# Later signs in the last block, a folded softmax sum, separate tiles for two convolution sums, and two matmul rounds moved ahead of a wait

## The chip, the cores and the metric

The kernel runs on one core of one Trainium2 chip. The metric is the time of one execution on the device in microseconds (us); the time before is 1892.93 us, the median of three runs from 1892.58 to 1893.13. The engines are named as in the profile: PE is TensorE (matmuls; PEld its weight loads), DVE is VectorE, ACT is ScalarE, POOL is GpSimd, SP is the engine whose queue issues most DMAs.

## The reference

The input x has 8 images of 64 channels and 64 x 64 pixels, float32. Two layers follow each other.

```
# layer 0: attention over the N = 4096 pixels of each image
q, k, v = wq @ x + bq, wk @ x + bk, wv @ x + bv
q, k = q - mean(q), k - mean(k)                       # means over pixels
out = softmax(q^T k / 8) applied to v  +  a unary term, one column per image
x = x + out
# layer 1: three binary convolutions and a gate
for kernel sizes 1, 3, 5:
    s += batchnorm(conv(sign(x + move), sign(w - mean(w)) * mean(|w|)))
gate = sigmoid(grouped linear map of the mean of s over pixels)   # one value per channel
out = s * gate + x
```

The gate needs the mean of s over the whole image, so no pixel of an image can be written before all of its convolutions have been summed, in one form or another.

## The kernel before

Two images lie on the 128 partitions (64 channels each), so there are four pairs of images. A pair's 4096 query pixels are cut into 8 blocks of 512 (8 image rows each); `attend` runs the 32 blocks one after the other.

**The rounds of a block.** A block has 32 rounds, one for each 128 keys. In a round `scores` makes the logits (L584) into a pair of PSUM banks, ScalarE takes their exponential into a tile `e` (L597; the pool `ep` has five of these), `weighted` multiplies the `e` of the round before with the values (L609) into the two banks `acc`, and `summed` adds the `e` of the round before to the running sum `es` on VectorE (L627, called a fold below). `weighted` and `summed` are one round behind `scores`.

**The plan.** Everything else is woven into the rounds by `plan`: `put(i, f, ...)` lists the function f to be issued in round i. For block g, the plan holds the steps that finish block g-1: the softmax sums go through DRAM (`gather`, `fold_first`, `fold`, `fold_last`, `spread`), then `added` (L719) joins the two halves of the attention output, `finish` (L723, L724) scales it and adds x, `signs_wide` (L762) and `signs` (L756) write the signs for the three convolutions on ScalarE and start the DMAs that copy them to the other image's partitions (L840, L757). Each engine works through its own queue in the order in which the instructions are issued, so a step's round decides what is queued behind it.

**The last block.** Block 31 is done in two parts, `PARTS`: a wide part of 384 query columns in 32 rounds, and a narrow part of 128 columns in 8 rounds of four key tiles each. `plan_last` takes the plan of block 31 and moves index i to i * 512 // 384, then puts its own steps. `NK` is 32, so `NK + n` is round n of the narrow part.

For the last pair the gate must be known before the convolutions of the last rows are summed. So the mean of s over rows 40 to 63 is taken from sums of signs along image rows: `row_sums(n, y0, y1)` reduces the signs of convolution n (0, 1, 2 for sizes 1, 3, 5) over rows y0 to y1 (L789) and corrects the ends (L795), and `gate_lines` multiplies these line sums with all taps (L809). `gate_mean` (L1125, L1127) sums what the earlier rows gave; `gate_lines_out` (L822), `gate_logits` and `gate_out` make the gate from both.

**The tail.** After the last round: `sums_wide` (L698) multiplies ones with the running sum `es` and with the last `e` to get the softmax sums of the narrow part; `reciprocals_wide` (L713) inverts them; the last `weighted` group follows, and `added_out` and `finish` give the last 128 pixels (rows 62 and 63). TensorE then runs the convolutions of blocks 5 and 6 (rows 40 to 55): `one` for the 1x1, `three` with 9 rounds and `five` with 25 rounds of four matmuls each, one round per tap (L1099). `out1` and `add` (L1113, L1118) bring them from PSUM into the sums; `store` (L1159) applies the gate and starts the output DMA. Last come rows 56 to 63 (block 7), for which the 3x3 and the 5x5 sums lie side by side in one PSUM tile of two banks:

```
t = ps_s.tile([P, 2, QB], F32, tag="s", name=f"z{p.name}_7")
w = QB // 2
z5, z3 = t[:, :, 0:w], t[:, :, w:]
```

L1557 adds all of z3 in one instruction, L1558 applies the gate, L1561 adds the 5x5 sums in two halves, and each half is stored by a DMA (L1563).

Of the kernel before, what the change touches and what calls it, by code (L numbers as in the profile page):

```python
# [18 lines left out]
F32 = mybir.dt.float32  # L19
# [3 lines left out]
ALU = mybir.AluOpType  # L23
# [3 lines left out]
P = 128  # L27
C = 64
HH = 64
N = HH * HH  # L30
KS = (1, 3, 5)
QB = 512
NQ = N // QB
NK = N // P
ROWS = QB // HH
# [13 lines left out]
def conv_seq_kernel(ctx, tc, x, wqv, wk, wv, w1, w3, w5, wtap, gw, out):  # L49
    nc = tc.nc  # L50
    n_pairs = x.shape[0] * x.shape[1] // P
    xf = x.rearrange("b c h w -> (b c) (h w)")
    of = out.rearrange("b c h w -> (b c) (h w)")
# [9 lines left out]
    ps_s = ctx.enter_context(tc.tile_pool(name="ps_s", bufs=2, space=PSUM))  # L63
# [3 lines left out]
    def m_tile(name):  # L67
        return ps_m.tile([P, QB], F32, tag="m", name=name)
# [4 lines left out]
    def load_x(name, rows, queues=(nc.sync,)):  # L73
        xt = x_tile(name)
        for c in range(4):
            cols = bass.ts(c, N // 4)
            queues[c % len(queues)].dma_start(out=xt[:, cols], in_=xf[rows, cols])
        return xt
# [118 lines left out]
    scale = cp.tile([P, 3], F32, tag="scale", name="scale")  # L197
# [82 lines left out]
    class Pair:  # L280
# [407 lines left out]
                )  # L688


        def sums_wide(self, qb, part=(slice(0, QB), 1), more=None):
            cols, n = part
            w = cols.stop - cols.start
            sums = m_tile(f"su_{self.name}_{qb}_{cols.start}")
            es = [self.es.pop(qb)] + ([] if more is None else [more])
            for i in range(n * len(es)):
                for b in range(2):
                    nc.tensor.matmul(  # L698
                        sums[img[b], 0:w],
                        ones[:, 0:C],  # L700
                        es[i // n][:, b, i % n * w : (i % n + 1) * w],
                        start=(i == 0),
                        stop=(i == n * len(es) - 1),
                    )
            self.sums_p = sums, cols.start

# [575 lines left out]
    def banks(pool, tag):  # L1282
        def two(name):
            t = pool.tile([P, 2, QB], F32, tag=tag, name=name)
            return [t[:, 0, :], t[:, 1, :]]

        return two

    quarters = [slice(c * N // 4, (c + 1) * N // 4) for c in range(4)]
    score_banks = banks(ps_s, "s")  # L1290
# [4 lines left out]
    def acc_banks(name):  # L1295
        return [ps_a.tile([P, QB], F32, tag=f"acc{h}", name=f"{name}_{h}") for h in range(2)]
# [5 lines left out]
    def rows_of(pr):  # L1302
        return slice(pr * P, (pr + 1) * P)

    def attend(pairs, early):
# [3 lines left out]
        def block(g):  # L1309
            return pairs[g // NQ], g % NQ  # L1310
# [4 lines left out]
        def plan(g):  # L1315


            at = {}

            def put(i, f, *a):  # L1320
                at.setdefault(i, []).append((f, a))

            pr, qb = divmod(g, NQ)
# [4 lines left out]
            if g >= 1:  # L1328
                p, b = block(g - 1)
# [28 lines left out]
            if g >= 1:  # L1358
                put(5, p.fold_first, b)
                put(6, p.fold, b)  # L1360
                put(7, p.fold_last, b)
                put(8, p.spread, b)
                put(9, p.check_block, b, 0)
                put(11, p.check_block, b, 1)
                last = g == n_blocks - 1
                put(11 if last else 13, p.added, b)
                put(12 if last else 15, p.finish, b)
                put(13 if last else 16, p.signs_wide, b, 2)
                put(13 if last else 18, p.signs_wide, b, 1)
                put(14 if last else 20, p.signs, b)  # L1370
            if g + 2 < n_blocks:
                put(2, lambda: block(g + 2)[0].copy_x(block(g + 2)[1], (g + 2) // NQ * P))
            if 2 <= g < n_blocks - 1:
# [33 lines left out]
            if pr + 1 < n_pairs:  # L1407
# [10 lines left out]
                if qb == 3:  # L1418
                    for c in range(8):
                        cols = slice(c * QB, (c + 1) * QB)  # L1420
                        put(14 + 2 * c, lambda c=c, cols=cols: nx().mean_part(c, cols, True))
                    put(30, lambda: nx().mean_sum(8))
                if qb >= 4:
                    for h in range(2):
                        i = 2 * (qb - 4) + h
# [8 lines left out]
        def plan_last():  # L1434

            at, (first, _) = {}, PARTS
            for i, steps in plan(n_blocks - 1).items():
                at[i * QB // first[0].stop] = steps

            def put(i, f, *a):  # L1440
                at.setdefault(i, []).append((f, a))

            p, b = pairs[-1], NQ - 1
            cols = first[0]
            r1 = cols.stop // HH
            put(4, p.begin_lines)
            for i, n in enumerate((2, 1, 0)):
                put(5 + i, p.row_sums, n, L0 - pads[n], 48)
                put(19 + i, p.row_sums, n, 48, 56)
            put(24, p.gate_mean)  # L1450
            put(NK, p.weighted_out, b, cols)
            put(NK + 1, p.added, b, cols)
            put(NK + 1, p.sums_wide, b, first)
            put(NK + 1, p.reciprocals_wide, b, cols)
            put(NK + 2, p.finish, b, cols)
            put(NK + 3, lambda: p.check(p.r[b][:, cols], n_blocks - 1))
            put(NK + 4, p.signs_wide, b, 2, 0, r1)
            put(NK + 5, p.signs_wide, b, 1, 0, r1)
            put(NK + 5, p.row_sums, 2, 56, 56 + r1)
            put(NK + 6, p.signs, b, 0, r1)  # L1460
            return at

        for g in range(n_blocks):
            pr, qb = divmod(g, NQ)
            last = g == n_blocks - 1
            at = plan_last() if last else plan(g)
            p = pairs[pr]
            parts = PARTS if last else ((slice(0, QB), 1),)
            steps = [(part, j) for part in parts for j in range(NK // part[1])]
            for i, (part, j) in enumerate(steps):  # L1470
                first = g == 0 and j < len(early)
                e = early[j] if first else p.scores(qb, j, None, part)
# [10 lines left out]
        p, b = pairs[-1], NQ - 1  # L1483

        def run(rounds):
            for f in rounds:
                f()

        part = PARTS[1]
        cols = part[0]  # L1490
        r0, r1 = cols.start // HH, ROWS
        y0, y1 = N // HH - ROWS + r0, N // HH
        rows_p = rows_of(n_pairs - 1)
        p.sums_wide(b, part, pending[1][2])
        p.row_sums(1, N // HH - ROWS, y0)
        p.row_sums(0, N // HH - ROWS, y0)
        p.reciprocals_wide(b, cols)
        pending[0].weighted(*pending[1], pending[2])
        z1, z5 = score_banks(f"z{p.name}_1"), score_banks(f"z{p.name}_5")
        z3 = []  # L1500
        halves = p.rows(NQ - 3), p.joint_rows(0, ROWS)
        one, three, five, out1, add = p.last_rows(halves, z1, z3, z5)
        one()
        p.added_out(b, cols)
        for side in range(2):
            p.check(p.r[b][:, cols], n_pairs * (NQ + 1), (side,))
        p.finish(b, cols)
        z3 += acc_banks(f"z{p.name}_3")
        run(five[0:2])
        run(three)  # L1510
        nb_ = sm.tile([P, 1], F32, tag="nb", name="nb")
        nc.vector.tensor_reduce(nb_, fit, AX.XY, ALU.add)
# [11 lines left out]
        out1(1)  # L1524
        add(1, 0)
        p.gate_lines_out()
        run(five[2:4])
        p.gate_logits()
        pb = m_tile("pb")
        nc.tensor.matmul(pb[:, 0:1], ones, nb_, start=True, stop=True)  # L1530
        run(five[4:])
        add(1, 1)
        good = sm.tile([P, 1], I32, tag="good", name="good")
        nc.vector.tensor_copy(good, pb[:, 0:1])
# [1 line left out]
        by = sm.tile([P, 1], F32, tag="nb", name="by")  # L1536
# [4 lines left out]
            add(2, h)  # L1541
            p.store(NQ - 3 + h, rows_p)

        t = ps_s.tile([P, 2, QB], F32, tag="s", name=f"z{p.name}_7")
        w = QB // 2
        z5, z3 = t[:, :, 0:w], t[:, :, w:]
        z1 = m_tile(f"z{p.name}_7_1")
        for i in range(2):
            p.conv_tap(p.joint_rows(ROWS, 2 * ROWS), [[z1]], i, 0, 0, 0, True, True)
        halves = [p.joint_rows(ROWS + h * ROWS // 2, ROWS + (h + 1) * ROWS // 2) for h in range(2)]  # L1550
        _, three, five, *_ = p.last_rows(halves, None, [z3[:, h] for h in range(2)], [z5[:, h] for h in range(2)])
        run(three)
        run(five)
        s = p.s[NQ - 1]
        nc.scalar.activation(s, z1, AF.Identity, bias=shift, scale=scale[:, 0:1])
        sv = s.rearrange("p (h w) -> p h w", w=w)
        nc.vector.scalar_tensor_tensor(sv, z3, scale[:, 1:2], sv, ALU.mult, ALU.add)  # L1557
        nc.vector.scalar_tensor_tensor(s, s, p.gt, p.x2[NQ - 1], ALU.mult, ALU.add)  # L1558
        for h in range(2):
            sh = sv[:, h, :]  # L1560
            nc.vector.scalar_tensor_tensor(sh, z5[:, h, :], by, sh, ALU.mult, ALU.add)  # L1561
            at = N - QB + h * w
            nc.sync.dma_start(out=of[rows_p, at : at + w], in_=sh)  # L1563
        return good

    with tc.manual_schedule():
# [30 lines left out]
        first.early_unary()  # L1597
        mix((first, 1), None)
        good = attend([first] + [None] * (n_pairs - 1), early)


# [3 lines left out]
    with tc.If(n_good < P):  # L1605
        neg = fp.tile([P, QB], F32, tag="t5", name="neg")
        nc.vector.memset(neg, 0.0)
        with tc.For_i(0, n_pairs * P, P) as row:
            rows = bass.ds(row, P)
            p = Pair("g", load_x("g", rows, (nc.scalar,)))  # L1610
# [11 lines left out]
            for qb in range(NQ):  # L1622
                mix((p, qb), None)
                for h in range(QB // P):
                    part = sm.tile([P, 2, NQ], F32, tag="part", name=f"part_{qb}_{h}")
                    for kb_ in range(NQ):
                        ps = ps_s.tile([P, 2, QB], F32, tag="s", name=f"px_{qb}_{h}_{kb_}")
                        for b in range(2):
# [5 lines left out]
                                stop=True,  # L1634
# [12 lines left out]
                for j in range(NK):  # L1647
                    e = p.scores(qb, j, neg)
# [75 lines left out]
```

## Time and profile before

| what | value |
|---|---|
| median of three runs | 1892.93 us |
| the profiled execution, its own time | 1892.65 us |
| its span, first to last instruction | 1890.8 us |
| PE busy | 1874.5 us, 99% |
| DVE busy | 1608.7 us, 85% |
| ACT busy | 1265.6 us, 67% |
| POOL busy | 130.1 us, 7% |
| mean granted TensorE clock | 0.999 |
| HBM traffic | 68 GB/s over the span |

A busy TensorE here means that a matmul was in flight. The page also follows the chain of work that ended last back to the start: TensorE holds 90% of it, and the two largest lines are L584 and L609, the attention's matmuls, with 43% each. Stretches of the last 111 us (busy us of each engine and number of instructions in it, granted clock, share of the DMA engines, GB/s):

```profile
1800.00:1820.00 20.00, 19.88 (x334) 9.81 (x330) 17.49 (x32) 13.71 (x20) 0.86 (x1) 1.00 0.27 55
1820.00:1840.00 20.00, 16.13 (x184) 7.18 (x179) 18.92 (x32) 11.21 (x19) 0.00 (x0) 0.91 0.11 32
1840.00:1850.00 10.00, 10.00 (x132) 4.71 (x124) 7.58 (x11) 6.25 (x8) 0.00 (x0) 1.00 0.01 2
1850.00:1860.00 10.00, 10.00 (x275) 7.64 (x268) 7.27 (x10) 5.97 (x7) 2.35 (x1) 1.00 0.02 4
1860.00:1870.00 10.00, 9.69 (x313) 9.13 (x308) 8.65 (x13) 6.81 (x12) 0.00 (x0) 1.00 0.13 30
1870.00:1880.00 10.00, 10.00 (x243) 6.62 (x238) 8.34 (x27) 3.73 (x11) 1.47 (x5) 1.00 0.27 97
1880.00:1891.00 11.00, 3.89 (x138) 3.62 (x128) 5.27 (x8) 0.78 (x1) 0.00 (x0) 0.92 0.31 113
```

The columns after the stretch and its length are PE, PEld, DVE, ACT and POOL. The wide part of the last block runs from about 1804 to 1853, the narrow part to about 1867, and the tail from there.

### The profile page before, as it was taken

What the parts mean: (1) busy time and instruction counts of PE and PEld (TensorE: products, weight loads), DVE (VectorE), ACT (ScalarE), POOL (GpSimd) and SP (SyncE); (2) the same over time, 40 slices, a digit from 0 to 9 for tenths busy, and PEclk for the clock granted to TensorE, in tenths of its full rate; (3) what the DMA queues carried; (4) which work ended last, traced back from release to release, by engine and by line L of the source; (5) the groups of instructions that cost most, each with busy time, mean ns of one, the idle gap of its engine ahead of it and who ended that gap; (6) DMA issues with size and microseconds to landing.
All of it is one profiled execution on the core that took longest, in us unless ns stands there. A gap on an engine that the chain in (4) does not pass through costs nothing.

```text
span 1890.8 us, 51550 instructions
## 1 busy us (share of the span) xinstructions
PE 1874.5 (99%) x22088; PEld 796.0 (42%) x22088; DVE 1608.7 (85%) x2548; ACT 1265.6 (67%) x1622; POOL 130.1 (7%) x176
## 2 busy tenths in 40 slices
PE   9999999999999999999999999999999999999998
PEld 4344344343344434443434444444433344444446
DVE  7888888889888888888888898888888888888887
ACT  6666776666666676666666667666666666666664
POOL 0000000000000000000000000000000000000000
PEclk9999999999999999999999999999999999999999
DMA  4234333333333433233333444233333333333311
GB/s 127 64 68 97 82 66 72 67 58 72 67 71 88 117 82 82 65 73 66 58 72 67 94 115 89 58 81 67 71 68 57 73 78 88 89 72 66 84 37 54
DMA packets 74004, 142.81 MB, mean 76 GB/s; under 512 B 10540, under 2 KB 42152, under 8 KB 73640
## 3 DMA queue, kind: packets, MB, share of 16 engines
q0 software_dynamic: 22320, 81.27, 23.3%
q1 hardware_dynamic: 51160, 57.58, 10.4%
q8 instruction: 174, 2.85, 0.6%
q10 hardware_dynamic: 288, 0.60, 0.1%
q14 instruction: 62, 0.51, 0.1%
HBM read 39.27 MB, written 89.78 MB: 68 GB/s over the span
## 4 chain that ended last, share of the span: by engine, by line
PE 90%; DMA 1%; ACT 0%; DVE 0%; issue 0%; ACTq 0%; DVEq 0%
PE ps L584 43%; PE acc L609 43%; PE z L968 2%; DMA es<-e 1%; PE z L1099 1%; PE pv L416 1%; PE pq L565 1%; PE z_5e L968 0%; ACT e L597 0%; PE su L698 0%; DVE es L627 0%; PE z L1058 0%; PE po L463 0%; PE zl L809 0%; ACT s L762 0%
## 5 line engine op out<-in xcount | busy, mean ns | idle before, releaser
L597 ACT ACTIVATE e<-ps 128x1024 f32<-128x1024 f32 (+1 forms) x1030 | 1047.6, 1017 | 566.9 <-PE ps L584 548.7
L627 DVE TENSOR_TENSOR es<-es,e 128x1024 f32<-128x1024 f32 (+1 forms) x841 | 1018.8, 1211 | 194.7 <-ACT e L597 181.7
L609 PE MATMUL acc<-e,v 64*64 64x512 f32 (+2 forms) x8432 | 1084.9, 577 | 6.2 <-ACT e L597 6.2
L584 PE MATMUL ps<-q,x 64*64 64x512 f32 (+2 forms) x8448 | 1089.6, 578 | 0.8 <-DVE q L349 0.8
L609 PEld LDWEIGHTS acc<-e,v 64*64 64x64 f32 x8432 | 333.3, 131 | 553.6 <-ACT e L597 321.0
L584 PEld LDWEIGHTS ps<-q,x 64*64 64x64 f32 x8448 | 357.0, 133 | 485.2 <-issue 264.1
L648 POOL DMA_DIRECT2D es<-e x93 | 80.0, 861 | 905.1 <-ACT e L597 600.0
L1038 DVE SCALAR_TENSOR_TENSOR sb<-pt,sb 128x256 f32<-128x256 f32 x174 | 65.9, 419 | 0.0
L968 PEld LDWEIGHTS <-wc 64*64 64x64 bf16 x3364 | 58.8, 106 | 1.7 <-issue 0.8
L648 POOL DMA_DIRECT2D es<-es x31 | 26.6, 857 | 438.7 <-DVE es L627 438.7
L625 DVE TENSOR_TENSOR es<-e,e 128x1024 f32<-128x1024 f32 (+1 forms) x31 | 37.7, 1216 | 17.2 <-ACT e L597 17.2
L968 PE MATMUL z<-ec,wc 64*64 64x128 bf16 x1392 | 51.4, 217 | 0.0
L968 PE MATMUL z<-t,wc 64*64 64x128 bf16 x1392 | 51.0, 216 | 0.1
L762 ACT ACTIVATE s<-x,wqv_s 128x512 bf16<-128x512 f32 (+2 forms) x66 | 46.1, 702 | 3.6 <-DVE x L724 3.5
L1001 ACT ACTIVATE pt<-z,frac 128x256 f32<-128x256 f32 (+1 forms) x58 | 30.5, 577 | 16.9 <-PE z L968 16.9
L646 POOL DMA_DIRECT2D es<-e x31 | 17.5, 564 | 334.2 <-ACT e L597 323.0
L635 DVE COPY o<-acc 128x512 f32<-128x512 f32 (+1 forms) x32 | 22.0, 687 | 9.8 <-PE acc L609 9.7
L1012 DVE TENSOR_TENSOR pt<-pt 128x384 f32<-128x384 f32 x58 | 29.6, 552 | 0.0
L416 PEld LDWEIGHTS pv<-wx,x 64*64 64x64 f32 x992 | 21.5, 134 | 16.1 <-issue 8.6
L663 DVE TENSOR_TENSOR e_parts<-e_parts 128x512 f32<-128x512 f32 x31 | 21.3, 687 | 6.6 <-DMA e_parts<-es 6.6
L724 DVE SCALAR_TENSOR_TENSOR x<-x,ou,x 128x512 f32<-128x512 f32 (+2 forms) x33 | 24.3, 735 | 1.2
L424 ACT COPY v<-pv 128x512 f32<-128x512 f32 x31 | 18.2, 586 | 8.7 <-PE pv L416 8.7
(206 smaller groups left out, 888.7 us busy)
## 6 DMA issues: line engine op xcount, KB each, us to landing
es<-e POOLq DMA_DIRECT2D x124, 512.0 KB, 5.1
es<-es POOLq DMA_DIRECT2D x31, 512.0 KB, 5.2
e_parts<-es SPq DMA_DIRECT2D x124, 128.0 KB, 2.9
r<-rc SPq DMA_DIRECT2D x62, 128.0 KB, 2.8
out<-sb SPq DMA_DIRECT2D x29, 256.0 KB, 2.2
x<-in_x SPq DMA_DIRECT2D x24, 256.0 KB, 4.1
ec<-t SPq DMA_DIRECT2D x29, 99.0 KB, 4.5
xc<-in_x SPq DMA_DIRECT2D x30, 72.0 KB
```

The costliest lines, as they stand in the source:

```text
L416: nc.tensor.matmul(pv[img[h], b, i * w : (i + 1) * w], self.x[img[b], bass.ds((4 * g + i) * P + h * H, H)], self.wx[img[b], 0:w], start=Tr ...
L584: nc.tensor.matmul(ps[img[h], b, i * w : (i + 1) * w], self.x[img[b], bass.ds((n * j + i) * P + h * H, H)], self.q[qb][img[b], cols], star ...
L597: nc.scalar.activation(e, ps[:, :, 0 : n * w], AF.Exp, scale=1.0 / 8.0)
L609: nc.tensor.matmul(self.acc[qb][h][img[b], 0:w], self.v[img[h], t, img[b]], e[img[h], b, at : at + w], start=(t == 0), stop=(t == NK - 1),)
L625: begin.tensor_tensor(self.es[qb], self.first, e, ALU.add)
L627: nc.vector.tensor_tensor(self.es[qb], self.es[qb], e, ALU.add)
L648: nc.gpsimd.dma_start(out=out, in_=e, accum_op=ALU.add)
L762: nc.scalar.activation(sy[n][0][:, rows, pad : pad + HH], self.x2[qb][:, r0 * HH : r1 * HH].rearrange("p (h w) -> p h w", w=HH), AF.Sign, ...
L968: nc.tensor.matmul(z[img[b], :].rearrange("p (q w) -> p q w", w=HH), wc[k][img[h], n, c * C : c * C + C], src[:, first : first + step + 1 ...
L1001: nc.scalar.activation(out, z, AF.Identity, scale=frac[:, by : by + 1])
L1012: nc.vector.tensor_tensor(self.pairs[:, :, :, r, :], t[:, 0:3, 0], t[:, 0:3, 1], op)
L1038: nc.vector.scalar_tensor_tensor(out, x, by, out, ALU.mult, ALU.add, **gap)
```

## The change

All of it lies in the last block and the tail; the other 31 blocks are issued as before.

- **Signs at later rounds.** For block 31's plan, `finish` goes from index 12 to 13, the 5x5 signs from 13 to 15, the 3x3 signs from 13 to 16, the 1x1 signs from 14 to 17; `added` stays at 11. In rounds these are 16 to 17, 17 to 20, 17 to 21 and 18 to 22. The row sums of rows 48 to 55 go from rounds 19, 20, 21 to 22, 23, 24, and `gate_mean` from 24 to 18. The row sums of the 5x5 signs of rows 56 to 61 go from round 5 of the narrow part to round 6.
- **A folded sum.** A new function, `fold_parts`, adds on VectorE the four quarters of `es` into one quarter (two instructions, 256 and then 128 columns of each image). `sums_wide` then takes the last `e` first, in four groups as before, and `es` in one group in place of four.
- **Two rounds in the wait.** The first two taps of the 5x5 are issued ahead of `fold_parts` and `sums_wide`, so their PSUM tile is taken first; the other places where taps of the 5x5 are issued go on from there. The 1x1 row sums of rows 56 to 61 move from behind `sums_wide` to behind `finish`.
- **Separate tiles.** For rows 56 to 63 the 3x3 sums go to the two `acc` banks and the 5x5 sums to a score tile of their own; the 3x3 sums are added in two halves.

```diff
+        def fold_parts(self, qb, w, n):
+            es = self.es[qb]
+            while n > 1:
+                n //= 2
+                nc.vector.tensor_tensor(
+                    es[:, :, 0 : n * w], es[:, :, 0 : n * w], es[:, :, n * w : 2 * n * w], ALU.add
+                )
...
-            es = [self.es.pop(qb)] + ([] if more is None else [more])
-            for i in range(n * len(es)):
+            es = self.es.pop(qb)
+            data = [es[:, :, i * w : (i + 1) * w] for i in range(n if more is None else 1)]
+            if more is not None:
+                data = [more[:, :, i * w : (i + 1) * w] for i in range(n)] + data
+            for i, e in enumerate(data):
                 for b in range(2):
                     nc.tensor.matmul(
                         sums[img[b], 0:w],
                         ones[:, 0:C],
-                        es[i // n][:, b, i % n * w : (i % n + 1) * w],
+                        e[:, b, :],
...
                 put(11 if last else 13, p.added, b)
-                put(12 if last else 15, p.finish, b)
-                put(13 if last else 16, p.signs_wide, b, 2)
-                put(13 if last else 18, p.signs_wide, b, 1)
-                put(14 if last else 20, p.signs, b)
+                put(13 if last else 15, p.finish, b)
+                put(15 if last else 16, p.signs_wide, b, 2)
+                put(16 if last else 18, p.signs_wide, b, 1)
+                put(17 if last else 20, p.signs, b)
...
                 put(5 + i, p.row_sums, n, L0 - pads[n], 48)
-                put(19 + i, p.row_sums, n, 48, 56)
-            put(24, p.gate_mean)
+                put(22 + i, p.row_sums, n, 48, 56)
+            put(18, p.gate_mean)
...
-            put(NK + 5, p.row_sums, 2, 56, 56 + r1)
+            put(NK + 6, p.row_sums, 2, 56, 56 + r1)
...
+        z3, z5 = [], score_banks(f"z{p.name}_5")
+        z1 = []
+        halves = p.rows(NQ - 3), p.joint_rows(0, ROWS)
+        one, three, five, out1, add = p.last_rows(halves, z1, z3, z5)
+        run(five[0:2])
+        p.fold_parts(b, cols.stop - cols.start, part[1])
         p.sums_wide(b, part, pending[1][2])
         p.row_sums(1, N // HH - ROWS, y0)
-        p.row_sums(0, N // HH - ROWS, y0)
         p.reciprocals_wide(b, cols)
         pending[0].weighted(*pending[1], pending[2])
-        z1, z5 = score_banks(f"z{p.name}_1"), score_banks(f"z{p.name}_5")
-        z3 = []
-        halves = p.rows(NQ - 3), p.joint_rows(0, ROWS)
-        one, three, five, out1, add = p.last_rows(halves, z1, z3, z5)
+        z1 += score_banks(f"z{p.name}_1")
         one()
         p.added_out(b, cols)
         for side in range(2):
             p.check(p.r[b][:, cols], n_pairs * (NQ + 1), (side,))
         p.finish(b, cols)
+        p.row_sums(0, N // HH - ROWS, y0)
         z3 += acc_banks(f"z{p.name}_3")
-        run(five[0:2])
+        run(five[2:4])
         run(three)
...
-        run(five[2:4])
+        run(five[4:6])
         p.gate_logits()
...
-        run(five[4:])
+        run(five[6:])
...
-        t = ps_s.tile([P, 2, QB], F32, tag="s", name=f"z{p.name}_7")
         w = QB // 2
-        z5, z3 = t[:, :, 0:w], t[:, :, w:]
-        z1 = m_tile(f"z{p.name}_7_1")
+        _, z5 = (ps_s.tile([P, 2, QB], F32, tag="s", name=f"z{p.name}_{n}") for n in ("none", "7_5"))
+        z1, z3 = m_tile(f"z{p.name}_7_1"), acc_banks(f"z{p.name}_7_3")
...
-        sv = s.rearrange("p (h w) -> p h w", w=w)
-        nc.vector.scalar_tensor_tensor(sv, z3, scale[:, 1:2], sv, ALU.mult, ALU.add)
+        for h in range(2):
+            add(1, h)
         nc.vector.scalar_tensor_tensor(s, s, p.gt, p.x2[NQ - 1], ALU.mult, ALU.add)
         for h in range(2):
-            sh = sv[:, h, :]
-            nc.vector.scalar_tensor_tensor(sh, z5[:, h, :], by, sh, ALU.mult, ALU.add)
-            at = N - QB + h * w
-            nc.sync.dma_start(out=of[rows_p, at : at + w], in_=sh)
+            add(2, h, by)
+            at = bass.ts(h, w)
+            nc.sync.dma_start(out=of[rows_p, bass.ds(N - QB + h * w, w)], in_=s[:, at])
```

More of the change, by code (lines that the diff above doesn't have):

```diff
@@ L700, in sums_wide @@
                         ones[:, 0:C],
-                        es[i // n][:, b, i % n * w : (i % n + 1) * w],
+                        e[:, b, :],
                         start=(i == 0),
-                        stop=(i == n * len(es) - 1),
+                        stop=(i == len(data) - 1),
                     )
@@ L1550, in attend @@
         halves = [p.joint_rows(ROWS + h * ROWS // 2, ROWS + (h + 1) * ROWS // 2) for h in range(2)]
-        _, three, five, *_ = p.last_rows(halves, None, [z3[:, h] for h in range(2)], [z5[:, h] for h in range(2)])
+        _, three, five, _, add = p.last_rows(halves, None, [z[:, 0:w] for z in z3], [z5[:, h, 0:w] for h in range(2)])
         run(three)
```

## The prediction

> **What bounds the kernel now.** I read the page first (its chain is 90% TensorE, so a change is worth what it does to TensorE's waits or to the work after its last matmul), then the waits of the last 96 us, where every edited line runs, then the timeline of three places there. The waits (engine, line, what it waited for: us in total, times, longest):
>
> ```profile
> PE acc L609 <- ACT e L597: 3.9, 1, 3.9
> ACT s L762 <- DVE x L724: 3.5, 1, 3.5
> ...
> DVE es_j L1557 <- PE z L1099: 1.1, 1, 1.1
> ...
> PE su L698 <- DVE es L627: 0.3, 1, 0.3
> ```
>
> The first two are one event, in round 17 of the last block's wide part (384 columns, a round is 1.29 us of TensorE). Its timeline (start, duration, engine, line, operation; in brackets the idle time before):
>
> ```profile
> 1827.52 0.81 ACT L597 ACTIVATE e<-ps 128x768 f32<-128x768 f32 x1 [0.48 <-PE ps L584]
> ...
> 1828.38 2.01 DVE L627 TENSOR_TENSOR es<-es,e 128x768 f32<-128x768 f32 x2
> ...
> 1830.32 0.69 DVE L723 TENSOR_TENSOR x<-x,r 128x512 f32<-128x512 f32 x1
> 1831.04 0.75 DVE L724 SCALAR_TENSOR_TENSOR x<-x,ou,x 128x512 f32<-128x512 f32 x1
> ...
> 1831.83 1.34 ACT L762 ACTIVATE s<-x,wqv_s 128x512 bf16<-128x512 f32 x2 [3.49 <-DVE x L724]
> ...
> 1833.91 0.97 PE L609 MATMUL acc<-e,v 64*64 64x384 f32 x8 [3.87 <-ACT e L597]
> ```
>
> ScalarE has finished the exponential of round 17 at 1828.33; the next thing in its queue is the sign of the block before, which needs `finish` (L723, L724), and VectorE is two folds (L627) behind. So ScalarE stands 3.49 us, and TensorE 3.87 us. VectorE is busy throughout: the reader should see that the wait is VectorE's backlog, shown one engine on. At the wide part's end VectorE has caught up and waits again (timeline of VectorE alone, as in the next fence):
>
> ```profile
> 1852.22 0.96 DVE L627 TENSOR_TENSOR es<-es,e 128x768 f32<-128x768 f32 x1 [0.33 <-ACT e L597]
> 1853.57 0.56 DVE L635 COPY o<-acc 128x384 f32<-128x384 f32 x1 [0.39 <-PE acc L609]
> 1854.32 0.56 DVE L719 TENSOR_TENSOR x<-o,o 128x384 f32<-128x384 f32 x1 [0.20 <-ACT o L634]
> 1856.29 2.58 DVE L713 RECIPROCAL r<-su 128x128 f32<-128x128 f32 x3 [1.41 <-PE su L698]
> ```
>
> And the end, where VectorE waits for the last 5x5 tap before it touches even the 3x3 sums:
>
> ```profile
> 1879.97 0.75 DVE L1118 SCALAR_TENSOR_TENSOR sb<-z,scale,sb 128x512 f32<-128x512 f32 x1 [0.68 <-PE z L1099]
> ...
> 1884.02 0.75 DVE L1557 SCALAR_TENSOR_TENSOR es_j<-z,scale,es_j 128x512 f32<-128x512 f32 x1 [1.06 <-PE z L1099]
> 1884.81 0.75 DVE L1558 SCALAR_TENSOR_TENSOR es_j<-es_j,gt,x 128x512 f32<-128x512 f32 x1
> 1885.59 0.88 DVE L1561 SCALAR_TENSOR_TENSOR es_j<-z,by,es_j 128x256 f32<-128x256 f32 x2
> ```
>
> [...] after the 3.87 us wait the granted clock was 0.64 and 0.51 in the next two 2 us windows, while after a 1.28 us wait near 160 us it stayed 1.00; and the exponential queued behind the waiting sign did not pass it. [...] The old layout put the 3x3 and 5x5 sums of a half in one bank, which fits L1557's wait although its own taps ended about 3 us earlier.
>
> **Part 1: signs at later rounds.** Plan index i becomes round i x 512 // 384. `finish` goes from round 16 to 17, the signs from 17, 17, 18 to 20, 21, 22. Removed: TensorE's 3.87 us wait, and the slow clock behind it: the next four groups of 8 matmuls took 0.97 + 1.28 + 1.28 + 0.97 = 4.50 us in the chain where four normal ones take 4 x 0.645 = 2.58, so 1.92 more; 5.79 together.
>
> What is late next? Unstalled, the exponential of round 20 ends at 1827.52 + 3 x 1.29 + 0.81 = 1832.20. VectorE starts folds at 1828.38, 1829.44, 1830.50 (1.06 apart back to back, from the 2.01 for two), then L723 at 1831.38, L724 at 1832.10, end 1832.85. So the first sign still waits 0.7, the exponential of round 21 starts 0.8 late, of which 0.44 is spare (1.27 from an exponential's start to its matmuls, less 0.83): TensorE stands 0.4. TensorE alone would be 5.4 earlier.
>
> But VectorE's queue up to L635, the copy that frees the bank for the narrow part's first weighted matmuls, has the same contents as before (`gate_mean`, 0.3, comes earlier in it; the row sums change rounds and not number). It was idle there only in waits that the stall gave it. Starts to starts, without waits, from 1828.38: three folds to L723 1.06 + 1.06 + 0.88; `finish` 0.72 + 0.67; fold, `gate_mean` and on 0.88 + 0.34; folds 18 to 21, 3 x 1.06; folds with row sums 1.91, 1.68 and 1.50 (before: 1833.89 to 1835.80 to 1837.48; the third 0.87 + about 0.63); folds 24 to 31, 7 x 1.06; last fold to L635 0.88. Sum 22.2, so L635 starts at 1850.6 instead of 1853.57. TensorE restarts when the 0.56 copy is over, at 1851.2, not 1854.34: a gain of 3.15, not 5.4. The other 2.2 us become a TensorE wait before the narrow part. [...] I take no clock drop (bounds 0 and the 1.9 lost before). The exponentials keep ahead: with five `e` buffers round j needs fold j-5, and the tightest, round 28, would start near 1842.6 with fold 23 done at 1841.8. The moved copy DMAs of the signs (SP, five of about 0.55 us issue) are needed only by the tail's taps; SP has nothing else between 1835.6 and 1862.9.
>
> In the narrow part (32-matmul groups of 0.87) TensorE, ScalarE and VectorE do what they did, VectorE's reciprocals through its last fold being continuous already; `row_sums(2, 56, 62)` passes one fold, and the queue to the last fold is the same length. Everything shifts by 3.15.
>
> **Part 2: two rounds in the wait, and the fold.** Times here are those of before, the shift left out. Removed: TensorE's 0.31 wait and 32 matmul records of L698, 1.97. In their place from 1866.97: two 5x5 taps, 2 x 0.22 (eight matmuls; TensorE's taps start 0.22 apart at 1870.8 to 1872.8), the newest `e` in 16 records, 1.0, and a wait for VectorE. That adds 128x512, 0.69 (L663's), and 128x256, 0.41 (L668's), with 0.1 of dependence each: 1867.29 to 1868.55. The last 4 records take 0.25, the weighted group 1.03: accumulators end at 1869.88, not 1870.33, and two taps are already done. The taps' copied signs were issued by 1863.4 and land in 2.0, so they do not wait.
>
> VectorE: row sums of the 3x3 to 1869.26, reciprocal (0.96) to 1870.15, `added_out` 1870.23, `finish` ending 1871.23 (0.45 early); but now the 1x1 row sum (0.55, hidden under L698 before) follows, then the counters, and the last `row_sums(2)` ends at 1872.91 instead of 1872.84. TensorE is through `one`, two taps and the 3x3 at about 1872.6 and waits until 1872.95 for those lines; before it began them at 1872.98. So of this part only the two taps remain, 0.03 + 0.44 = 0.47: the 5x5 ends at 1879.45, VectorE's last store before it at 1879.27, and L1118's wait falls from 0.68 to 0.2.
>
> **Part 3: separate tiles.** VectorE is through its stores at 1882.96 - 0.47 = 1882.49. The 3x3 sums no longer wait: two 128x256 adds 0.88 (as L1561), the gate step 0.05 + 0.78, two last adds 0.88: end 1885.04, TensorE being through at 1883.46. Before: 1886.47. The gain of parts 2 and 3 is 1.43, of which the split costs 0.13 (two adds for one) and saves 1.06. If it saved nothing new, the end would be bounded by TensorE, 1883.46 + 2.5: still 0.47. The last output DMAs and the 4.3 us after VectorE's end are the same.
>
> **Sum.** 3.15 + 1.43 = 4.6. The profiled execution took 1892.65 (span 1890.8 and 1.85 around it): 1888.05; the median of the runs is 0.28 above it: **1888.3**. A measurement of this kernel can tell about 0.2%, 3.8 us, from no change, so the border is 1889.1.
>
> **Rivals.**
> - *VectorE is not the bound*: its back-to-back spacing shrinks and TensorE gets all of 5.4, with 1.43: 6.8, 1886.1. Against: 2.01 or 2.02 for two folds recurs four times from 1809 on.
> - *The clock drops once before the narrow part*: [...] 1.9 is lost again: 1890.2. [...] Against: the 1.28 us wait left no trace in the clock.
> - *The tail gives nothing*: the taps placed ahead of the sums, or the row lines, meet a late tile (the 5x5 banks of the tail being held until L1118 at 1882.2, for one): only 3.15, 1889.8.
> - *Slower*: the slow clock does not recover in the narrow part[...]. Each us at half clock loses 0.5. The part runs 16 us at full speed; from 9 us of slow clock the gain is gone, and if it holds for 16 us, half of the part's work, 8 are lost: 1892.9 - 4.6 + 8 = 1896.3. Against: before, TensorE was busy for 10.72 of the 11.0 us from 1856.3, at clock 1.00.
>
> **How the numbers follow.** Forecast 0.66 (own range 1887.2 to 1889.2), VectorE not bound 0.11, clock 0.08, tail 0.10, slower 0.05. Unknowns of the forecast: the fold spacing (16 of them, 0.05 each way, 0.8) and the tail's waits (0.5). Range 1886.2 to 1890.4: it takes in the clock and tail rivals and half of the first. Faster by over 0.2%: 0.62 of the forecast, 0.11, and 0.03 from edges, 0.76; same 0.19; slower 0.05.
>
> **What would show it.** Right: no ScalarE wait of over 1 us on L724; clock 1.00 to the end; VectorE without waits from about 1828 to L635 at 1850.6; a TensorE wait of about 2 us before the narrow part; a small wait at the line matmuls (L809's successor); the last VectorE operation near 1881.9. Wrong: folds waiting for exponentials in the wide part, slow matmuls in the narrow part, or VectorE still waiting for TensorE before the last 3x3 adds.

## The result and the profile after

The changed kernel takes 1887.99 us, the median of 11 runs (1886.57 to 1889.4), against 1893.13 (1892.4 to 1894.41) of the kernel before on the same chip: a ratio of 0.9971, 95% interval 0.9962 to 0.998. The forecast was 1888.3. A second set of runs beside the last experiments gave 1888.01 (18 runs) against 1892.31: 0.9978 (0.9971 to 0.9985). That the first median lies 0.3 us from the forecast is in part luck: the median of the kernel before alone was 1892.93, 1893.13 and 1892.31 in the three sets, so the gain is 5.1 us by one set and 4.3 by the other.

Single runs of one kernel lie up to 5.5 us apart, and the profiles show part of this ahead of every edited line: the place where the last block begins falls anywhere from 1802.3 to 1806.3 us. So all profiles below are read from an anchor that no edit moves, the start of VectorE's 512-column accumulator copy at the beginning of the last block (1803.87 us before, 1804.14 after). Two profiles of the changed kernel agree from there within 0.02 us up to VectorE's end and within 0.05 at the end of the span. Kernels that keep TensorE's 3.87 us wait agree less well: L635 starts at 48.02 in the tail-only run and at 49.70 before, with a granted clock of 1.00 behind the wait in the one and of 0.64 and 0.51 in the other.

| us from the anchor | before | after | gained up to here |
|---|---|---|---|
| VectorE's copy L635 starts | 49.70 | 46.59 | 3.11 |
| first reciprocal during the narrow part (of the wide part's sums) | 52.42 | 49.27 | 3.15 |
| end of VectorE's last fold | 63.40 | 60.24 | 3.16 |
| first add of the 5x5 of rows 40 to 55 | 76.10 | 72.24 | 3.86 |
| end of VectorE's last operation | 82.60 | 77.79 | 4.81 |
| end of the span | 86.93 | 82.06 | 4.87 |

The waits of the last 92 us of the changed kernel (engine, line, what it waited for: us in total, times, longest; lines after the edited functions have moved down by 11, so L735 is the old L724, L773 the old L762, L709 the old L698, L1129 the old L1118; L695 is in `fold_parts`):

```profile
PE acc L609 <- DVE o L635: 1.4, 1, 1.4
...
ACT s L773 <- DVE x L735: 0.8, 2, 0.7
...
PE acc L609 <- ACT e L597: 0.5, 1, 0.5
...
DVE sb L1129 <- PE z L1110: 0.2, 1, 0.2
...
PE su L709 <- DVE es L695: 0.2, 1, 0.2
```

ScalarE's wait of 3.5 us is down to 0.7, TensorE's of 3.9 to 0.5, and a new one stands first: TensorE waits for VectorE's copy. The place of the old stall, in time:

```profile
1831.65 0.69 DVE L734 TENSOR_TENSOR x<-x,r 128x512 f32<-128x512 f32 x1
...
1832.37 0.75 DVE L735 SCALAR_TENSOR_TENSOR x<-x,ou,x 128x512 f32<-128x512 f32 x1
...
1833.04 0.95 DVE L627 TENSOR_TENSOR es<-es,e 128x768 f32<-128x768 f32 x1
...
1833.16 0.72 ACT L773 ACTIVATE s<-x,wqv_s 128x512 bf16<-128x512 f32 x1 [0.69 <-DVE x L735]
...
1833.79 0.79 ACT L597 ACTIVATE e<-ps 128x768 f32<-128x768 f32 x1
```

The exponential again starts behind the sign that is ahead of it in ScalarE's queue. In the kernel before, the exponential of round 18 stood behind two signs and started 4.32 us after its logits' matmuls had ended at 1828.75:

```profile
1827.92 0.83 PE L584 MATMUL ps<-q,x 64*64 64x384 f32 x8
...
1833.07 0.79 ACT L597 ACTIVATE e<-ps 128x768 f32<-128x768 f32 x1
```

And the end of the wide part, in VectorE's timeline and then the other engines':

```profile
1842.42 8.39 DVE L627 TENSOR_TENSOR es<-es,e 128x768 f32<-128x768 f32 x8
1850.73 0.55 DVE L635 COPY o<-acc 128x384 f32<-128x384 f32 x1
1851.39 2.10 DVE L730 TENSOR_TENSOR x<-o,o 128x384 f32<-128x384 f32 x1
1853.41 2.56 DVE L724 RECIPROCAL r<-su 128x128 f32<-128x128 f32 x3
```

```profile
1850.72 2.35 POOL L625 TENSOR_TENSOR es<-e,e 128x1024 f32<-128x1024 f32 x1 [45.54 <-ACT e L597]
...
1849.54 0.43 PE L609 MATMUL acc<-e,v 64*64 64x128 f32 x2
1851.34 1.10 PE L609 MATMUL acc<-e,v 64*64 64x128 f32 x30 [1.36 <-DVE o L635]
```

In the kernel before, TensorE did not wait at that place:

```profile
1854.34 1.10 PE L609 MATMUL acc<-e,v 64*64 64x128 f32 x32
```

In the changed kernel no line of VectorE above has a wait in brackets: eight folds run back to back, where each had waited 0.33 us before. L730 is the old L719; it took 0.56 us before and 2.10 now, of which more below. The tail, in VectorE's timeline:

```profile
1876.38 0.75 DVE L1129 SCALAR_TENSOR_TENSOR sb<-z,scale,sb 128x512 f32<-128x512 f32 x1 [0.25 <-PE z L1110]
...
1879.28 0.87 DVE L1129 SCALAR_TENSOR_TENSOR es_j<-z,scale,es_j 128x256 f32<-128x256 f32 x2
1880.19 0.75 DVE L1571 SCALAR_TENSOR_TENSOR es_j<-es_j,gt,x 128x512 f32<-128x512 f32 x1
1881.05 0.88 DVE L1129 SCALAR_TENSOR_TENSOR es_j<-z,by,es_j 128x256 f32<-128x256 f32 x2
```

The 3x3 adds of the last rows wait for nothing, and VectorE works to its end.

### The profile page after: what moved, and what is told of

Its sections match the earlier page's. It is cut to its first block, busy times and chain, and to the rows that moved or that the text cites. A ratio compares the mean times of both kernels' runs of the same rounds, so it can differ in the third digit from the quotient of the medians.

```text
span 1886.2 us, 51530 instructions
## 1 busy us (share of the span) xinstructions
PE 1873.3 (99%) x22076; PEld 794.9 (42%) x22076; DVE 1611.0 (85%) x2551; ACT 1265.5 (67%) x1622; POOL 130.1 (7%) x176
## 3 DMA queue, kind: packets, MB, share of 16 engines
q8 instruction: 174, 2.85, 0.6%
## 4 chain that ended last, share of the span: by engine, by line
PE 89%; DVE 2%; DMA 1%; ACT 0%; issue 0%; DVEq 0%; ACTq 0%
PE ps L584 42%; PE acc L609 42%; PE z L979 2%; DVE es L627 1%; DMA es<-e 1%; PE pv L416 1%; PE pq L565 1%; PE z L1110 0%; PE z_5e L979 0%; ACT e L597 0%; DVE es_j L1129 0%; PE z L1069 0%; DVE vu_lines L800 0%; ACT rc_ck L523 0%; PE po L463 0%
## 5 line engine op out<-in xcount | busy, mean ns | idle before, releaser
L773 ACT ACTIVATE s<-x,wqv_s 128x512 bf16<-128x512 f32 (+2 forms) x66 | 46.2, 702 | 0.8 <-DVE x L735 0.8
L635 DVE COPY o<-acc 128x512 f32<-128x512 f32 (+1 forms) x32 | 22.0, 687 | 9.4 <-PE acc L609 9.3
L735 DVE SCALAR_TENSOR_TENSOR x<-x,ou,x 128x512 f32<-128x512 f32 (+2 forms) x33 | 24.3, 736 | 1.2
```

What stands on the lines that cost most here:

```text
L773: nc.scalar.activation(sy[n][0][:, rows, pad : pad + HH], self.x2[qb][:, r0 * HH : r1 * HH].rearrange("p (h w) -> p h w", w=HH), AF.Sign, ...
```

## The experiments

Theory V says that VectorE's queue bounds the last block once the stall is gone; theory T, the rival, that the stall was the cost and VectorE has room. The times before are those of the kernel before beside each run, on the same chip. All readings are from the anchor unless a run's time is named.

**The signs alone.** The kernel before with the edits of `plan` and `plan_last`, as in the first part of the diff.

> The kernel before with the later signs alone. Theory V (VectorE's queue carries the last block once the stall is gone): 3.1 us less than before; the copy L635 starts near 1850.7 instead of 1853.57 with VectorE's idle time gone, and TensorE waits 1.3 to 2.2 us for it before the narrow part. Rival T (the stall of ScalarE and TensorE was the whole cost and VectorE has room): 5.4 us less, L635 near 1848, no such wait.

Measured: 1889.77 us against 1892.64 before, ratio 0.9985 (0.9978 to 0.9992). L635 starts at 46.58, the first reciprocal at 49.27, both as in the whole change and 3.1 us ahead of before; TensorE waits 1.35 us for the copy. From L635 to VectorE's end it takes 32.86 us, before 32.90: this part does nothing in the tail. V holds, T falls.

**The tail alone.** The changed kernel with the old rounds:

```diff
-                put(13 if last else 15, p.finish, b)
-                put(15 if last else 16, p.signs_wide, b, 2)
+                put(12 if last else 15, p.finish, b)
+                put(13 if last else 16, p.signs_wide, b, 2)
...
```

> The changed kernel with signs, row sums and gate_mean back at their old rounds: folded sum, two rounds ahead of the sums and separate tiles alone. V: 1.4 to 1.7 us less than before, and with the 3.1 of the signs alone the two add up to the whole change. Rival: the tail's edits pay only because the signs moved, so that this one gives under 0.7 us.

Measured: 1890.75 us, ratio 0.999 (0.9981 to 0.9998), 1.9 us less than before. L635 to VectorE's end takes 31.26 us, 1.64 less than before and as in the whole change (31.20): the two parts add up. But L635 itself starts at 48.02, 1.68 earlier than before, though TensorE's stall has the same 3.87 us. Up to the tail this kernel has the instructions of before in their old order. What differs is the granted clock after the stall, shown below: 1.00 here, 0.64 and 0.51 before.

**The separate tiles alone.** The last part of the diff in the kernel before (with one score tile, since the tiles are taken in the old order).

> The kernel before with separate tiles for the 3x3 and 5x5 sums of rows 56 to 63 alone. Working of the prediction: 0.9 us less; the first 128x256 add starts as soon as VectorE is through its store, 1.0 us earlier than L1557 did, and VectorE then ends 2.6 us after that store instead of 3.5. Rival: TensorE's last matmul and the adds behind it set the end, so nothing is gained: 0.

Measured: 1891.68 us, ratio 0.9997 (0.9988 to 1.0005), no difference that the times can tell. The profile can: from the first 5x5 add of rows 40 to 55 to VectorE's end it takes 5.54 us, before 6.50. So 0.96 is gained, as worked out. The edit gives the two sums both other tiles and other banks, so which of the two VectorE's wait hung on is not shown; that it was the shared bank was the author's estimate.

**The copy on ScalarE.** In the changed kernel:

```diff
-            nc.vector.tensor_copy(self.o[qb][1][:, cols], acc[1][:, 0:w])
+            copy = nc.scalar.copy if w < QB else nc.vector.tensor_copy
+            copy(self.o[qb][1][:, cols], acc[1][:, 0:w])
```

> The changed kernel with the wide part's second accumulator copy (L635) on ScalarE, which is idle there for over 3 us. V: TensorE restarts the narrow part right behind its scores, its sums then wait only for the last fold, and the first reciprocal starts about 1.7 us earlier: 1.7 us less than the changed kernel, 6.3 to 6.8 less than before. Rival T: VectorE's queue is not what TensorE waits for, so no change against the changed kernel, or 0.5 us more for the second copy on ScalarE.

Measured: 1885.34 us (5 runs), ratio 0.9962 to before (0.9948 to 0.9976). The first reciprocal comes at 47.72, 1.55 earlier than in the changed kernel, and VectorE ends at 76.26, 1.53 earlier; the span ends only 0.9 earlier: from VectorE's end to the end of the span it takes 4.9 us instead of 4.3, and what takes longer there is not shown. This is the shortest median of all versions. It was not timed on one chip with the changed kernel, and the intervals of the two ratios overlap; that it is ahead of that kernel rests on the profiles and on its five runs (1885.17 to 1887.37).

**The same copy in the kernel before.** The same edit there is the counter-check.

> The kernel before with the wide part's second accumulator copy on ScalarE. V: there VectorE had caught up and waited for TensorE, so its copy cost nothing; two copies in a row on ScalarE restart TensorE 0.2 to 0.5 us later, so 0 to 0.5 us more than before. Rival (the copy is dear wherever it runs on VectorE): 1.2 us less, as in the changed kernel.

Measured: 1893.27 us against 1892.64, ratio 0.9999 (0.9991 to 1.0008). The first reciprocal is at 52.79, 0.37 later. The copy is worth 1.5 us only where VectorE is behind: this is the point on which V and T differ most, and V holds.

**Signs one index later still.**

```diff
-                put(15 if last else 16, p.signs_wide, b, 2)
-                put(16 if last else 18, p.signs_wide, b, 1)
-                put(17 if last else 20, p.signs, b)
+                put(16 if last else 16, p.signs_wide, b, 2)
+                put(17 if last else 18, p.signs_wide, b, 1)
+                put(18 if last else 20, p.signs, b)
...
-                put(22 + i, p.row_sums, n, 48, 56)
+                put(23 + i, p.row_sums, n, 48, 56)
```

> The changed kernel with the signs one index later still (16, 17, 18) and the row sums of rows 48 to 55 one round later. V: ScalarE's wait of 0.7 us on L735 and TensorE's of 0.4 go, and nothing comes of it, because VectorE's queue up to L635 is as long as before: L635 within 0.2 us of where it was, time within 0.3 us of the changed kernel. T: 0.4 us less.

Measured: 1888.56 us (13 runs). ScalarE's wait is gone and L635 starts at 46.59, the same to the hundredth: as V says. But the first reciprocal comes at 49.82, 0.55 late, and VectorE ends 1.27 late. TensorE's wait before the narrow part has grown to 2.08 us, and after it the clock is low. Stretches of 2 us (the third figure from the end, before the DMA share and GB/s, is the granted clock):

```profile
1850.00:1852.00 2.00, 0.54 (x20) 0.54 (x24) 1.90 (x3) 0.05 (x1) 1.86 (x1) 1.00 0.00 0
1852.00:1854.00 2.00, 2.00 (x30) 0.65 (x18) 1.56 (x1) 0.00 (x0) 1.15 (x1) 0.62 0.02 4
1854.00:1856.00 2.00, 2.00 (x42) 2.00 (x44) 1.91 (x3) 0.00 (x0) 0.00 (x0) 0.53 0.03 8
```

The sums of the wide part then take 1.55 us instead of 0.87. So this run shows the prediction's clock rival at work, in a kernel that differs by one index, and it is why the expectation that nothing comes of the edit fails in this profile.

**The same kernel once more.**

> The changed kernel with the signs one index later, a second look at the clock after its TensorE wait of 2.1 us. If the length of the wait decides, half clock follows again and the first reciprocal comes 0.55 us later than in the changed kernel; [...] it may come without, and then within 0.1 us of the changed kernel.

Measured: the wait is 2.07 us, and this time the clock stays at 1.00:

```profile
1852.00:1854.00 2.00, 1.91 (x38) 1.14 (x42) 1.90 (x2) 0.00 (x0) 1.78 (x1) 1.00 0.02 4
1854.00:1856.00 2.00, 2.00 (x76) 2.00 (x80) 2.00 (x4) 0.92 (x1) 0.00 (x0) 1.00 0.03 8
```

The first reciprocal comes at 49.22 and VectorE ends at 77.73, within 0.1 us of the changed kernel. The length of the wait does not decide alone. The longer wait of before shows the same: in two of the three experiments that keep it (the separate tiles, and the copy in the kernel before), half clock follows it as in the kernel before (a granted clock of 0.50 in one 2 us stretch of each, 0.51 before), and in the tail-only run, where TensorE restarts at 1834.93, none does:

```profile
1832.00:1834.00 2.00, 0.00 (x0) 0.00 (x0) 1.86 (x4) 1.15 (x2) 0.00 (x0) 1.00 0.00 0
1834.00:1836.00 2.00, 1.07 (x16) 0.51 (x16) 1.83 (x3) 2.00 (x4) 0.00 (x0) 1.00 0.30 70
1836.00:1838.00 2.00, 2.00 (x32) 0.91 (x28) 1.93 (x5) 1.17 (x3) 0.00 (x0) 1.00 0.42 100
```

**Without the fold.** The changed kernel with `es` in four groups and no `fold_parts`:

```diff
-            data = [es[:, :, i * w : (i + 1) * w] for i in range(n if more is None else 1)]
+            data = [es[:, :, i * w : (i + 1) * w] for i in range(n)]
...
-        p.fold_parts(b, cols.stop - cols.start, part[1])
```

> The changed kernel without fold_parts, the running sum in four groups again (the same sums in another order). TensorE's 12 more records take 0.74 us and the wait of 0.2 and the tail of VectorE's two adds go: 0.3 us more than the changed kernel, all of it carried to the end. Rival (VectorE's two adds of 1.15 us cost what the records save): 0 or less.

Measured: 1888.16 us (8 runs), which the times cannot tell from the changed kernel. From the end of the last fold to the first 5x5 add it takes 12.27 us, with `fold_parts` 12.00: the fold is worth 0.27.

**Without the two rounds ahead.** The changed kernel with the first two 5x5 taps behind the sums:

```diff
-        run(five[0:2])
         p.fold_parts(b, cols.stop - cols.start, part[1])
...
-        run(five[2:4])
+        run(five[0:2])
         run(three)
...
```

> The changed kernel with the first two 5x5 taps behind the sums again. In the changed kernel the sums waited for ScalarE's last exponential even behind the taps, so the taps were free there: without them 0.44 us more, seen as VectorE's wait at the first 5x5 add going from 0.25 to 0.7 us. Rival (the taps delayed the sums as much as they saved): 0.

Measured: 1888.25 us (13 runs), again within the scatter; but the same stretch takes 12.44 us, 0.44 more, and VectorE's wait at the first 5x5 add is 0.68 instead of 0.25. The two taps were free where they stand.

**Copies on ScalarE and signs later, and with GpSimd's help.** First the two edits above together:

> The changed kernel with the copies on ScalarE and the signs one index later, without GpSimd. V: the sums of the wide part then wait for VectorE's last fold, which ends where it did; the first reciprocal comes at most 0.15 us earlier than with the copies alone. Rival T: 0.7 us earlier.

Measured: 1888.14 us (13 runs); the first reciprocal is at 49.22, 1.5 us later than with the copies alone. Neither theory had this. The timeline of VectorE and GpSimd shows it:

```profile
1851.48 2.72 DVE L731 TENSOR_TENSOR x<-o,o 128x384 f32<-128x384 f32 x1
1854.12 2.57 DVE L725 RECIPROCAL r<-su 128x128 f32<-128x128 f32 x3
```

```profile
1850.93 2.85 POOL L625 TENSOR_TENSOR es<-e,e 128x1024 f32<-128x1024 f32 x1 [44.97 <-ACT e L597]
```

VectorE's add of two SBUF tiles (`added`, here L731) is under way for as long as GpSimd adds two SBUF tiles, 2.72 us instead of 0.56. It ends 0.42 us after GpSimd's. With the copies alone VectorE began first and was not held; GpSimd, 0.15 us later, took 2.61 us instead of 2.35:

```profile
1851.02 0.55 DVE L731 TENSOR_TENSOR x<-o,o 128x384 f32<-128x384 f32 x1
```

```profile
1851.17 2.61 POOL L625 TENSOR_TENSOR es<-e,e 128x1024 f32<-128x1024 f32 x1 [45.70 <-ACT e L597]
```

In these profiles the one of the two adds that started later took longer than it did apart from the other, and `added` ended 0.42 us after GpSimd's both here and in the changed kernel, where it began 0.67 us behind the start of GpSimd's and took 2.10. GpSimd's 2.85 here began beside VectorE's last fold, which also adds two SBUF tiles and ended at 1851.56. What the two engines contend for is not shown. VectorE's instructions that read PSUM took no longer beside GpSimd's add: three reciprocals took 2.58 us in the kernel before, where GpSimd's add ran beside the first two, and 2.56 in the changed kernel behind it; the copy L635 took 0.55 in the changed kernel beside it and 0.56 before, ahead of it.

Then both with three folds of the wide part given to GpSimd:

```diff
+            elif e.shape[-1] == 384 and j == 20:
+                self.first = e
+            elif e.shape[-1] == 384 and j == 21:
+                self.es2 = self.tile(fp, "pt", "es2", (P, 14, 2 * HH))[:, 0:6, :].rearrange("p (b n) w -> p b (n w)", b=2)
+                nc.gpsimd.tensor_tensor(self.es2, self.first, e, ALU.add)
+            elif e.shape[-1] == 384 and j == 25:
+                nc.gpsimd.tensor_tensor(self.es2, self.es2, e, ALU.add)
...
+                if e.shape[-1] == 384 and j == 28:
+                    nc.vector.tensor_tensor(self.es[qb], self.es[qb], self.es2, ALU.add)
```

> Three things on top of the changed kernel: both wide accumulator copies on ScalarE, the signs one index later still, and three folds of the wide part (rounds 20, 21, 25) added on GpSimd into a dead tile that VectorE adds once, so VectorE has two folds less. V: with VectorE's queue 2.1 us shorter TensorE is the bound up to the first reciprocal, which comes 0.6 to 0.7 us earlier than with the copies alone; 6.9 to 7.6 us less than before, and no TensorE wait over 1 us near the narrow part, so no slow clock there. Rival (GpSimd's adds slow VectorE's down): no earlier than with the copies alone.

Measured: 1886.93 us (7 runs), 1.1 less than the changed kernel on the same chip (1888.01), though the intervals of the two ratios overlap; but the first reciprocal is at 47.99, 0.27 later than with the copies alone. The expectation was wrong: the exponentials now wait 1.2 us in two places for `e` buffers that the folds free late, TensorE 0.8 us for an exponential, and one of VectorE's small adds took 1.09 us beside GpSimd's instead of 0.18. Which of these costs the most was not taken apart. Near the narrow part TensorE did not wait, and the granted clock was 1.00 from 1848 to 1858.

**The changed kernel again.**

> The changed kernel once more, beside the two above on one chip, for the comparison of their times and for the clock: its wait before the narrow part of 1.36 us goes without a slow clock again, L635 to the end of VectorE takes 31.2 us again.

Measured: as stated at the top; the wait is 1.35 us, the clock 1.00 from 1848 to 1858, L635 to VectorE's end 31.21 us.

## Why the prediction held, and where its sum was off

The forecast was 4.6 us less, and VectorE's end comes 4.81 earlier by the anchor.

- *The stall goes and VectorE is late next.* Shown. The chain of starts gave L635 3.0 earlier, measured 3.11, and the first reciprocal 3.15 earlier, measured 3.15. ScalarE's remaining wait was put at 0.7 and is 0.69, TensorE's at 0.4 and is 0.45. The signs-only run and the copy moved in both kernels show that the gain ends at VectorE's queue.
- *The wait before the narrow part.* The mechanism is right, the size was off: 2.2 us expected, 1.36 measured. By starts, TensorE reached the narrow part's first weighted matmuls 5.07 us earlier than before, where 5.4 was counted: 0.7 went in the rounds in which ScalarE does a sign and an exponential (its exponential of round 20 starts at 1831.67, that of round 24 at 1837.53, 0.70 more than four rounds of 1.29), of which the prediction had 0.4. With the signs later, where ScalarE's wait is gone, it is 5.78, and 5.79 was reckoned for that. TensorE resumed 3.27 earlier (47.20 for 50.47), where 3.15 was counted. The last 0.4 is how a wait is counted: the profile starts it at the end of the two matmuls already issued, 0.43 us after the first of them began. It costs the forecast nothing, as VectorE decides there.
- *The narrow part shifts as it is.* Shown: 3.15 at its first reciprocal, 3.16 at its last fold. What the prediction did not see is that GpSimd's add now meets `added` and holds it for 1.5 us (2.10 for 0.56). It cost about 0.1 us: the reciprocal started at 1853.41, and TensorE's sums, begun at 1852.36 and lasting 0.87, were not there before 1853.23. So the exact 3.15 is in part luck: TensorE resumed 0.1 earlier than reckoned, and the hold took 0.1 back.
- *The kernel before loses 1.9 us to a slow clock.* So it did in its profile, at a granted clock of 0.64 and 0.51, and the prediction took it as fixed. The tail-only run has the stall without the slow clock, and its L635 comes at 48.02: against that, the later signs are worth 1.43 us there and not 3.11. What they save differs from run to run; over its runs the signs-only kernel was 2.9 us faster. Of the 32 runs of the kernel before that were timed beside the changed one, 23 had a mean granted clock of 0.998 or less, of the 18 of the changed kernel two; the mean does not say where in the run the clock was low.
- *Fold and taps, 0.47.* Measured 0.70 (12.70 to 12.00): the taps 0.44 as reckoned, the fold 0.27 where 0.03 was reckoned. The fold is the term that was mis-sized, by way of TensorE's path from the last weighted group to the line matmuls: 2.7 reckoned, 2.84 in the chain both before and after. With it, the row sums, which end 5.54 us after the last fold (5.62 reckoned), come just in time; the 0.35 us wait for them is in no view.
- *Separate tiles, 0.96 of the rest.* Measured 0.95 in the whole change and 0.96 alone.
- *Rivals.* That VectorE is not the bound is ruled out. The clock drop is real and its place was right (0.62 and 0.53 behind the 2.08 us wait of the later signs), but in all five profiles with the 1.35 or 1.36 us wait (the changed kernel twice, the signs alone, no fold, no taps) the clock stayed at 1.00. That none would follow the 2.2 us wait was the author's estimate: the profile of before had a drop behind a 3.87 us wait and none behind one of 1.28. A tail that gives nothing is ruled out by 1.65 us. Nothing of the slower case was seen in the changed kernel.

## What to carry to other kernels

When a stall of a few us on the bounding engine is taken away, add up the queue of the engine that caused it to the next point where the bound needs it: the stall had given that engine time to catch up, and only the shorter of the two gains was paid here, 3.15 us of TensorE's 5.07. Then move what sits at that point (here one 0.56 us copy) to an engine that is idle there; the same move was worth 1.5 us after the change and nothing before it. Compare such small gains between fixed instructions of two traces, where 0.3 us could be seen (0.27 for the fold) if the granted clock is the same in both, when whole times scatter by several us.

## What was not expected of the hardware

- The length of a TensorE wait did not decide alone whether half clock followed. It followed a 2.08 us wait once (a granted clock of 0.62 and 0.53 in the two 2 us stretches behind it) and not a 2.07 us wait of the same kernel (1.00); it followed the 3.9 us wait in three profiles of four (down to 0.51, 0.50 and 0.50; 1.00 in the tail-only run), and a wait of 1.35 or 1.36 us in none of five. What else decides is not shown. Where it fell, it cost 1.3 us at VectorE's end in the later-signs kernel, and between the tail-only run and before 1.68 us at L635.
- VectorE's busy time was longer beside GpSimd's add, with no wait shown: `added` on 128x384 took 0.56 in the kernel before, where GpSimd's add began 0.64 us after its end, and 2.10 and 2.72 where it began 0.67 and 0.55 behind the start of GpSimd's.
